# First tile of x on one queue with later loads held, first normalisations by column halves, first VectorE sums in other places

## The chip, the cores and the metric

One core of one Trainium2 chip. The metric is device time in microseconds (us), the median of several runs. The engines are named as in the profile: PE is TensorE (PEld its weight loads), DVE VectorE, ACT ScalarE, POOL GpSimd, SP SyncE, which issues most of the transfers. An engine works through its instructions in the order in which the program lists them.

## What is computed

x holds 2048 rows of 512 numbers (2 x 1024 x 512), all in fp32:

```python
xn = layernorm(x)                                  # per row, eps 1e-5
s  = xn @ (weight * block_mask).T                  # 512 x 512, 32 x 32 blocks
nx = xn * rsqrt(mean(xn * xn) + 1e-5) * ln_w
h  = silu(nx @ gate_w.T) * (nx @ up_w.T)           # 512 -> 1792
g  = silu(h @ down_w.T)                            # 1792 -> 512
out = x + s * g
```

## The kernel before, in words

**Tiling.** Rows are taken in four tiles `t` of 512, each as four pieces `i` of 128 rows by 512 columns (256 KB). A piece is normalised in place, transposed on PE by 128 x 128 blocks, and the four blocks of one column block `c` fill one PSUM bank `pt[t, c]`. From there ScalarE copies it out (`evacuate`, L158), or VectorE reads the bank directly in a sum.

**The products.** All matrix products are made by a scheme of seven products in place of eight, used twice, an outer one (`q`) over large blocks and an inner one (`m`) over small ones. It trades PE work for sums and differences of blocks, which VectorE and GpSimd make. `instance(j, ...)` (L333) is one outer product, with its seven inner ones in the order m = 1, 5, 2, 6, 3, 7, 4. Each inner product here is two matmul steps of 128 x 128 by 512, about 0.86 us together. They gather in banks `x`, `y` and `z` of the instance. After some of them a running value is copied away (`snap`, L358) or added to a total (`total`, L365). `seed` (L346) saves the first value of `x` as `s1` for the first two instances. `inner_b(q, m)` (L211) makes the operand sums of the x side, `inner_a` (L312) those of the weights, after `scale_a` (L266) has multiplied the weights by `ln_w`. Instances 0 and 1 need x tiles 0 and 1 only; tiles 2 and 3 come much later. The gate, up and attention products are 56 instances; after them come the down products (`down_instance`, L584) and the final sum.

**What sets the order.** Nothing is scheduled by the compiler. `at(pos, fn)` (L68) puts a function at a position; at the end all are called in the order of position, and ties in the order of entry. One position is one inner product, so instance j begins at 7 j. For the start, `T(us)` (L677) turns microseconds into positions, and `EARLY` (L678) moves the first products and sums of instances 0 and 1 to positions of their own. Waits follow from the data: whoever touches a buffer later waits for whoever touched it before.

**Names and lines that matter.**
- `load_x` (L118) issues the four pieces of a tile, for tile 0 two on SyncE and two on ScalarE. L681 to L691 list the first loads in SyncE's order: x tile 0, `ln_w`, weights of group 0 (two loads of 256 KB, `load_a`), x tile 1, weights of group 1, x tile 2, weights of group 2, x tile 3. `load_a` writes into the slots from `a1`.
- `constants` (L107) makes the identity matrix and others on GpSimd.
- `stats` (L124) is a bn_stats and a bn_aggr on VectorE for each piece; `factors` (L129) turns a tile's means and variances into scale and bias: VectorE, a square root on ScalarE, then two small VectorE instructions.
- `normalise` (L143) is one instruction for each piece, on ScalarE for pieces 0 and 1 and on VectorE for pieces 2 and 3.
- `RINGS` (L72) names the SBUF slots. `slot(tag)` takes them in turn; the rings `s2` and `s5` have two slots each, for the values that `snap` saves. `PSB` (L91) gives the PSUM banks: three for X, two for Y, one for Z, two for V. The first z of instance 1 lies in a Y bank, and so do `pt[0, 1]` and `pt[0, 2]`.
- `warm` (L698) is a row of products on the identity before the first data.

Of the kernel before, what the change touches and what calls it, by code (L numbers as in the profile page):

```python
# [10 lines left out]
AF = mybir.ActivationFunctionType  # L11
ALU = mybir.AluOpType
AX = mybir.AxisListType

P = 128
W = 512
# [15 lines left out]
def tile_masked_linear_gated_ffn(  # L32
# [35 lines left out]
    def at(pos, fn, *args):  # L68
        events.append((pos, len(events), fn, args))
# [23 lines left out]
    def bank(tag, name):  # L93
        return ps.tile([P, W], F32, tag=tag, name=name, bufs=PSB[tag])
# [23 lines left out]
    def load_x(t):  # L118
        for i in range(TT):
            xt[t, i] = mem[:, first_slot[("B6", "vc", "v5", "B4")[t]] + i, :]  # L120
            eng = nc.scalar if t == 0 and i >= 2 else nc.sync
            eng.dma_start(xt[t, i], x[(t * TT + i) * P : (t * TT + i + 1) * P, :])

    def stats(t, i):  # L124
        st = small.tile([P, 6], F32, tag="st", name=f"st_{t}_{i}")
# [14 lines left out]
        return [lambda: nc.vector.tensor_scalar(scl, agg[:, t, :, 1], 1.0 + EPS, EPS * EPS, ALU.mult, ALU.add),  # L140
                lambda: nc.scalar.activation(scl, scl, AF.Sqrt), last]

    def normalise(t, i, eng):  # L143
        scl, nb = stat[t]
        if eng is dve:
            nc.vector.tensor_scalar(xt[t, i], xt[t, i], scl[:, i : i + 1], nb[:, i : i + 1], ALU.mult, ALU.add)
            return
        nc.scalar.activation(xt[t, i], xt[t, i], AF.Identity, bias=nb[:, i : i + 1], scale=scl[:, i : i + 1])

    pt = {}  # L150

# [160 lines left out]
    def inner_a(g, part, k0=0, n=2):  # L312

        if part == 1:
            i, si, qs = F["a1"] + 2 * (g % 3), F["s"] + 2 * (g % 2), (1, 2)
        else:
            i, si, qs = *w_slots(g), BLOCKS
        a, s = slots(i + k0, n), slots(si + k0, n)
        a11, a21, a12, a22 = (a[:, :, k * P : (k + 1) * P] for k in range(4))
        s1, s2, s3, s4 = (s[:, :, k * P : (k + 1) * P] for k in range(4))  # L320
        for k in range(n):
            aop[g, qs[k0 + k]] = {1: a11[:, k], 2: a12[:, k], 3: s4[:, k], 4: a22[:, k],
                                  5: s1[:, k], 6: s2[:, k], 7: s3[:, k]}
        return [lambda: add(pool, s1, a21, a22), lambda: add(pool, s2, s1, a11, ALU.subtract),
                lambda: add(pool, s4, a12, s2, ALU.subtract), lambda: add(pool, s3, a11, a21, ALU.subtract)]
# [7 lines left out]
    def instance(j, g, q, prior, dest, after):  # L333


        st = {}

        seeded = j > 1

        def mm(m, tag, key, first):  # L340
            if first and key not in st:
                st[key] = bank("Y" if key == "z" and j == 1 else tag, f"{key}_{j}")
            nc.tensor.matmul(st[key], weights(g, q, m), operand(q, m), start=first and not (key == "z" and seeded),  # L343
                             stop=True, skip_group_check=True)

        def seed():  # L346

            if seeded:
                st["z"] = bank("Z", f"z_{j}")
                nc.scalar.copy(st["z"], st["x"])  # L350
            else:
                st["s1"] = slot("s2", f"s1_{j}")
                if prior is None:
                    nc.scalar.copy(st["s1"], st["x"])
                else:
                    add(dve, st["s1"], st["x"], prior(0))

        def snap(key, name, i):  # L358
            s = st[name] = slot(name, f"{name}_{j}")
            if prior is None:  # L360
                nc.scalar.copy(s, st[key])
            else:
                add(dve, s, st[key], prior(i))

        def total(key, name, i):  # L365
            if key == "z" and not seeded:
                name = "s1"
            if name:
                add(dve, dest(i), st[key], st[name])
            elif prior is None:  # L370
                nc.scalar.copy(dest(i), st[key])
            else:
                add(dve, dest(i), st[key], prior(i))

        at(EARLY.get((j, 0), 7 * j + 1), seed)
        for off, m, tag, first, snapshot, out in (
            (0, 1, "X", True, None, None),
            (2, 5, "Y", True, ("s5", 3), None),
            (3, 2, "Z", True, None, (None, 0)),
            (4, 6, "X", False, ("s2", 1), None),  # L380
            (6, 3, "Y", False, None, ("s2", 1)),
            (8, 7, "X", False, None, ("s5", 3)),
            (12, 4, "X", False, None, (None, 2)),
        ):
            key, pos = tag.lower(), 7 * j + off
# [198 lines left out]
    def down_instance(o, q, where_, prior, dest, after):  # L584
# [78 lines left out]
        if last_set:  # L663
            at(where_(17) + 0.1, base_of_last)
            for part, pos in zip(parts, (where_(23), where_(24), where_(25))):
# [8 lines left out]
    where = {gq: j for j, gq in enumerate(order)}  # L674
    N = len(order)
    END = 7 * N
    T = lambda us: (us - 14.9) / 0.86  # L677
    EARLY.update({(0, 1): T(11.5), (0, 0): T(12.6), (1, 1): T(12.7), (0, 2): T(12.8), (1, 2): T(12.9),  # L678
                  (1, 0): 4.5, (1, "z"): 7.0})
    SILU = 26.2  # L680
    at(T(-10), load_x, 0)  # L681
    at(T(-10), lambda: nc.sync.dma_start(lnw_sb, ln_w))
    for K in range(2):
        at(T(-10), load_a, 0, K)
    at(T(-10), load_x, 1)
# [3 lines left out]
    for K in range(2):  # L689
        at(T(-10), load_a, 2, K)  # L690
    at(T(-10), load_x, 3)  # L691
    at(T(-10), constants)
    def plan(pos, step, todo):
        for i, fn in enumerate(todo):
            at(pos + step * i, fn)


    def warm(n, b):  # L698
        for _ in range(n):
            nc.tensor.matmul(b[:, :P], ident, ident, start=True, stop=True, skip_group_check=True)  # L700

    at(T(1.4), lambda: warm(30, bank("V", "idle")))
    for t, p, step in ((0, T(8.2), 0), (1, T(13.4), 0), (2, 36.0, 1.2), (3, 36.1, 1.2)):
        plan(p, step, factors(t))
    for i in range(TT):
        half = act if i < 2 else dve
        at(T(4.5 + 0.85 * i), stats, 0, i)
        at(T(9.0 + 0.7 * (i % 2)), normalise, 0, i, half)
        at(T(10.1 + 0.8 * i), stats, 1, i)
        at(T(14.2 + 0.7 * (i % 2)), normalise, 1, i, half)  # L710
        for c in range(KC):
            at(T((10.2, 10.6, 11.0, 11.8)[c] + 0.1 * i), transpose, 0, c, (2, 3, 0, 1)[i], "XYYX"[c])
            at(T((15.3, 15.7, 16.1, 16.9)[c] + 0.1 * i), transpose, 1, c, (2, 3, 0, 1)[i], "XVVV"[c])
    at(T(6.0), scale_a, 0, 0, pool)
    at(T(8.2), scale_a, 0, 1, pool)
    for c in range(KC):
        at(T((10.7, 11.3, 11.9, 12.85)[c]), evacuate, 0, c, act)
        at((5.6, T(16.0), 6.0, 3.14)[c], evacuate, 1, c, act)
    for us, q, m, eng in ((15.9, 1, 5, dve), (16.6, 1, 6, dve), (17.2, 1, 7, dve), (17.8, 2, 5, dve), (18.4, 1, 4, pool),
                          (18.5, 2, 6, dve), (19.6, 2, 7, dve), (19.8, 2, 4, pool)):  # L720
        at(T(us), inner_b, q, m, eng)
    for q in (1, 2):
        for k in (0, 1):
            for n in (0, 1):
                at(8, outer_b, q, k, n, None)
    at(T(16.4), scale_a, 1, 0)
    at(5.2, scale_a, 1, 1)
    for i in range(TT):
        at(14.0 + 2.5 * i, stats, 2, i)
# [28 lines left out]
    for g in range(G + 1):  # L758
        p, rest = 7 * where[g, 1], 7 * where[g, BLOCKS[0]]
        for K in range(2):  # L760
            if g > 2:
                at(p - 22, load_a, g, K)
            if g == G:
                at(p - (10.4, 7.3)[K], lambda K=K: mask_a(aq[G, 0, K], 0, K))
            elif g > 1:
                at(p - (10.4, 7.3)[K], scale_a, g, K)
        if g:
            plan(p - 7, 1, inner_a(g, 1))
        else:
            plan(T(7.4), 0, inner_a(0, 1, 0, 1))  # L770
            plan(T(10.0), 0, inner_a(0, 1, 1, 1))
        at(rest - 29, load_block, g)

        def block_sums(g=g):
            for k, fn in enumerate(outer_a(g)):
                todo[g, k] = fn
        at(rest - 20, block_sums)
        if g == G:
            for k, (R, K) in ((1, (1, 0)), (4, (1, 1)), (0, (0, 0)), (3, (0, 1))):
                at(rest - 20.5, lambda k=k, R=R, K=K: mask_a(wblk[G][k], R, K))  # L780
        for k, off in enumerate((-19.9, -19.3, -18.1, -17, -15.95, -15.94, -15.93, -15.3, -13.95)):
            at(rest + off, lambda g=g, k=k: todo[g, k]())
        plan(rest - 13, 2.5, inner_a(g, 2, 0, 5))
# [138 lines left out]
```

## Time and profile before

| What | us |
|---|---|
| Median of 3 runs | 514.32 (514.15 to 514.35) |
| The profiled execution, own time | 514.33 |
| Its span, first to last instruction | 512.5 |
| Warm-up products on PE (L700), first start and busy time | 1.35, 8.37 |
| Factors of tile 0 on VectorE (L140), start | 8.06 |
| First transposes on PE (L155), start | 9.59 |
| The four early products `x`, `x`, `z`, `z` (L343), start | 11.59, 12.96, 13.82, 14.68 |
| The next ones `y`, `x`, `y`, `x`, `y`, start | 17.42, 18.97, 19.83, 20.96, 22.75 |
| Weight scaling on GpSimd (L262), two pairs, start | 6.89, 10.85 |
| Weight sums on GpSimd (L97), two sets of four, start | 8.80, 12.75 |

The table follows one execution through its first 23 us. Starts count from the span's start. The granted PE clock is full in all stages. The 1277 matmul records of the page are single steps; two of them make one inner product in the instances. PE records overlap, so a busy figure near the stretch's length means that one step follows another without a break, not that the array is at its peak. The transfers run without a break from 2.6 to about 17.5 us and then stop until 26; the 1.83 us between the span and the execution's own time lie around the program.

### The profile page before, as it was taken

What the parts mean: (1) busy time and instruction counts of PE and PEld (TensorE: products, weight loads), DVE (VectorE), ACT (ScalarE), POOL (GpSimd) and SP (SyncE); (2) the same over time, 40 slices, a digit from 0 to 9 for tenths busy, and PEclk for the clock granted to TensorE, in tenths of its full rate; (3) what the DMA queues carried; (4) which work ended last, traced back from release to release, by engine and by line L of the source; (5) the groups of instructions that cost most, each with busy time, mean ns of one, the idle gap of its engine ahead of it and who ended that gap; (6) DMA issues with size and microseconds to landing.
All of it is one profiled execution on the core that took longest, in us unless ns stands there. A gap on an engine that the chain in (4) does not pass through costs nothing. (4 is left out here: it accounts for less than half of the span.)

```text
span 512.5 us, 4939 instructions
## 1 busy us (share of the span) xinstructions
PE 506.2 (99%) x1277; PEld 231.2 (45%) x1277; DVE 380.8 (74%) x586; ACT 181.7 (35%) x344; POOL 340.5 (66%) x282
## 2 busy tenths in 40 slices
PE   8999999999999999999999999999999999999997
PEld 7444444444444444444444444444444444444444
DVE  5879689875987969789696978968847645367736
ACT  3566864642536344353634433331100101001111
POOL 5522223994695978869598789977652664739960
PEclk9999999999999999999999999999999999999999
DMA  8335645359159486685948567499997698467372
GB/s 310 142 123 215 245 156 217 153 226 329 60 220 334 165 297 233 230 299 209 315 181 296 205 246 258 156 334 390 352 345 269 198 382 320 146 255 220 145 230 83
DMA packets 60460, 121.59 MB, mean 237 GB/s; under 512 B 5760, under 2 KB 13328, under 8 KB 58384
## 3 DMA queue, kind: packets, MB, share of 16 engines
q1 hardware_dynamic: 60144, 120.75, 66.1%
q10 hardware_dynamic: 288, 0.52, 0.3%
q8 instruction: 10, 0.16, 0.1%
q14 instruction: 18, 0.15, 0.1%
HBM read 75.11 MB, written 46.15 MB: 237 GB/s over the span
## 5 line engine op out<-in xcount | busy, mean ns | idle before, releaser
L97 POOL TENSOR_TENSOR mem<-mem 128x512 f32<-128x512 f32 (+4 forms) x245 | 305.8, 1270 | 136.7 <-ACT mem L264 37.6
L343 PE MATMUL x<-mem 128*128 128x512 f32 x448 | 213.6, 594 | 0.3
L343 PEld LDWEIGHTS x<-mem 128*128 128x128 f32 x448 | 83.7, 190 | 106.9 <-issue 86.7
L97 DVE TENSOR_TENSOR mem<-x,mem 128x512 f32<-128x512 f32 x137 | 92.6, 684 | 42.2 <-PE x L343 41.1
L343 PE MATMUL y<-mem 128*128 128x512 f32 x224 | 114.6, 593 | 0.7 <-DVE mem L97 0.7
L97 DVE TENSOR_TENSOR mem<-mem 128x512 f32<-128x512 f32 (+3 forms) x60 | 75.6, 1266 | 7.2 <-PE dx L591 4.4
L591 PE MATMUL dx<-mem 128*128 128x512 f32 x174 | 78.3, 592 | 0.0
L97 DVE TENSOR_TENSOR mem<-y,mem 128x512 f32<-128x512 f32 x96 | 65.7, 684 | 10.0 <-PE y L343 8.7
L343 PEld LDWEIGHTS y<-mem 128*128 128x128 f32 x224 | 42.2, 190 | 53.3 <-issue 46.7
L350 ACT COPY z<-x 128x512 f32<-128x512 f32 x54 | 30.9, 573 | 97.8 <-PE x L343 93.3
L343 PE MATMUL z<-mem 128*128 128x512 f32 x112 | 57.1, 593 | 0.0
L591 PEld LDWEIGHTS dx<-mem 128*128 128x128 f32 x174 | 33.1, 190 | 41.6 <-issue 40.9
L591 PE MATMUL dy<-mem 128*128 128x512 f32 x98 | 44.5, 592 | 0.0
L409 ACT ACTIVATE gate<-mem 128x512 f32<-128x512 f32 x56 | 33.1, 601 | 25.4 <-DVE mem L97 21.0
L414 DVE TENSOR_TENSOR mem<-gate,mem 128x512 f32<-128x512 f32 x56 | 38.1, 681 | 5.1 <-POOL mem L97 4.3
L564 POOL TENSOR_TENSOR mem<-mem 128x512 f32<-128x512 f32 x16 | 24.3, 1516 | 15.4 <-DMA mem<-s_dram 15.1
L343 PEld LDWEIGHTS z<-mem 128*128 128x128 f32 x112 | 21.0, 190 | 25.3 <-issue 24.4
L574 ACT ACTIVATE silu<-mem 128x512 f32<-128x512 f32 x15 | 9.0, 602 | 64.6 <-DVE mem L97 48.3
L97 DVE TENSOR_TENSOR mem<-z,mem 128x512 f32<-128x512 f32 x41 | 28.0, 682 | 3.4 <-PE z L343 3.4
L591 PEld LDWEIGHTS dy<-mem 128*128 128x128 f32 x98 | 18.6, 190 | 23.4 <-issue 23.2
L97 DVE TENSOR_TENSOR mem<-dx,mem 128x512 f32<-128x512 f32 x16 | 11.0, 690 | 20.1 <-PE dx L591 20.1
L591 PE MATMUL dz<-mem 128*128 128x512 f32 x56 | 25.2, 592 | 0.0
(72 smaller groups left out, 286.8 us busy)
## 6 DMA issues: line engine op xcount, KB each, us to landing
h_dram<-mem SPq DMA_DIRECT2D x98, 256.0 KB, 2.1
mem<-h_dram SPq DMA_DIRECT2D x28, 768.0 KB, 6.7
mem<-in_gu SPq DMA_DIRECT2D x42, 256.0 KB, 4.0
acc_dram<-mem SPq DMA_DIRECT2D x8, 1024.0 KB, 4.1
mem<-acc_dram SPq DMA_DIRECT2D x8, 1024.0 KB, 6.0
s_dram<-mem SPq DMA_DIRECT2D x16, 256.0 KB, 4.4
mem<-s_dram SPq DMA_DIRECT2D x16, 256.0 KB, 6.7
mem<-in_x_t SPq DMA_DIRECT2D x16, 256.0 KB, 6.4
```

Source lines behind the costliest of these rows:

```text
L97: eng.tensor_tensor(o, a, b, op)
L343: nc.tensor.matmul(st[key], weights(g, q, m), operand(q, m), start=first and not (key == "z" and seeded), stop=True, skip_group_check=True)
L350: nc.scalar.copy(st["z"], st["x"])
L409: nc.scalar.activation(gate[key], t(), AF.Silu)
L414: nc.vector.tensor_mul(a(), gate[key], b())
L564: at_later.append(lambda: nc.gpsimd.tensor_tensor(s_tile, s_tile, rms_bc[t], ALU.mult))
L574: nc.scalar.activation(b[0][:, part], y[:, part] if source is None else source(), AF.Silu)
L591: nc.tensor.matmul(st[key], w(), b(), start=first and key != "z", stop=True, skip_group_check=True)
```

## The change

It has five parts, all in the first 23 us:
- All four pieces of x tile 0 are issued by SyncE; `ln_w` goes to ScalarE's queue. `constants` is listed first.
- GpSimd copies one column of piece 0 into the first `a1` slot. The first weight load, next on SyncE's queue, writes that slot and so waits until piece 0 has landed.
- `normalise` gets a range of columns. For tiles 0 and 1 it is called twice for each piece, for columns 0 to 255 and 256 to 511, first halves of both pieces before second halves.
- `s1` of instance 0 is taken from the ring `s5` instead of `s2`.
- Positions: `T` is shifted by 0.9 us, and the entries of the start are changed. The third early product is now m=1 of instance 1 and the second m=2 of instance 0. Both weight scalings stand before both sets of weight sums on GpSimd. On VectorE, the order after `inner_b(1, 5)`, `(1, 6)`, `(1, 7)` was `inner_b(2, 5)`, total of z 0, `inner_b(2, 6)`, s1 of instance 1, `inner_b(2, 7)`, total of y 0, total of z 1; it is now total of z 0, `inner_b(2, 5)`, s1 of instance 1, `inner_b(2, 6)`, total of z 1, total of y 0, `inner_b(2, 7)`. The warm-up has 26 products for 30.

```diff
-            eng = nc.scalar if t == 0 and i >= 2 else nc.sync
-            eng.dma_start(xt[t, i], x[(t * TT + i) * P : (t * TT + i + 1) * P, :])
+            nc.sync.dma_start(xt[t, i], x[(t * TT + i) * P : (t * TT + i + 1) * P, :])
...
-    def normalise(t, i, eng):
+    def normalise(t, i, eng, cols=slice(0, W)):
         scl, nb = stat[t]
+        v = xt[t, i][:, cols]
         if eng is dve:
-            nc.vector.tensor_scalar(xt[t, i], xt[t, i], scl[:, i : i + 1], nb[:, i : i + 1], ALU.mult, ALU.add)
+            nc.vector.tensor_scalar(v, v, scl[:, i : i + 1], nb[:, i : i + 1], ALU.mult, ALU.add)
             return
-        nc.scalar.activation(xt[t, i], xt[t, i], AF.Identity, bias=nb[:, i : i + 1], scale=scl[:, i : i + 1])
+        nc.scalar.activation(v, v, AF.Identity, bias=nb[:, i : i + 1], scale=scl[:, i : i + 1])
...
-                st["s1"] = slot("s2", f"s1_{j}")
+                st["s1"] = slot("s2" if j else "s5", f"s1_{j}")
...
-    T = lambda us: (us - 14.9) / 0.86
-    EARLY.update({(0, 1): T(11.5), (0, 0): T(12.6), (1, 1): T(12.7), (0, 2): T(12.8), (1, 2): T(12.9),
-                  (1, 0): 4.5, (1, "z"): 7.0})
+    T = lambda us: (us - 14.0) / 0.86
+    EARLY.update({(0, 1): T(10.4), (0, 2): T(11.3), (1, 1): T(12.1), (1, 2): T(13.0), (0, 0): T(11.5), (1, 0): 4.3,
+                  (0, "z"): 3.26, (1, "z"): 4.9})
     SILU = 26.2
+    at(T(-10), constants)
     at(T(-10), load_x, 0)
-    at(T(-10), lambda: nc.sync.dma_start(lnw_sb, ln_w))
+    at(T(-10), lambda: nc.scalar.dma_start(lnw_sb, ln_w))
+
+    at(T(-10), lambda: nc.gpsimd.tensor_copy(mem[:, F["a1"], 0:1], xt[0, 0][:, 0:1]))
...
-    at(T(1.4), lambda: warm(30, bank("V", "idle")))
-    for t, p, step in ((0, T(8.2), 0), (1, T(13.4), 0), (2, 36.0, 1.2), (3, 36.1, 1.2)):
+    at(T(1.4), lambda: warm(26, bank("V", "idle")))
+    for t, p, step in ((0, T(7.1), 0), (1, T(12.5), 0), (2, 36.0, 1.2), (3, 36.1, 1.2)):
...
-        at(T(4.5 + 0.85 * i), stats, 0, i)
-        at(T(9.0 + 0.7 * (i % 2)), normalise, 0, i, half)
-        at(T(10.1 + 0.8 * i), stats, 1, i)
-        at(T(14.2 + 0.7 * (i % 2)), normalise, 1, i, half)
+        at(T(3.7 + 0.82 * i), stats, 0, i)
+        at(T(9.35 + 0.82 * i), stats, 1, i)
+        for h, cols in enumerate((slice(0, W // 2), slice(W // 2, W))):
+            at(T(7.95 + 0.9 * h + 0.4 * (i % 2)), normalise, 0, i, half, cols)
+            at(T(13.45 + 0.9 * h + 0.4 * (i % 2)), normalise, 1, i, half, cols)
...
-    at(T(8.2), scale_a, 0, 1, pool)
+    at(T(6.1), scale_a, 0, 1, pool)
...
-        at((5.6, T(16.0), 6.0, 3.14)[c], evacuate, 1, c, act)
-    for us, q, m, eng in ((15.9, 1, 5, dve), (16.6, 1, 6, dve), (17.2, 1, 7, dve), (17.8, 2, 5, dve), (18.4, 1, 4, pool),
-                          (18.5, 2, 6, dve), (19.6, 2, 7, dve), (19.8, 2, 4, pool)):
-        at(T(us), inner_b, q, m, eng)
+        at((5.6, T(15.6), 6.0, 3.14)[c], evacuate, 1, c, act)
+    for pos, q, m, eng in ((1.1, 1, 5, dve), (1.87, 1, 6, dve), (2.56, 1, 7, dve), (3.95, 2, 5, dve), (2.7, 1, 4, pool),
+                           (4.6, 2, 6, dve), (7.2, 2, 7, dve), (5.0, 2, 4, pool)):
+        at(pos, inner_b, q, m, eng)
...
-    at(T(16.4), scale_a, 1, 0)
+    at(2.1, scale_a, 1, 0)
...
-            plan(T(7.4), 0, inner_a(0, 1, 0, 1))
-            plan(T(10.0), 0, inner_a(0, 1, 1, 1))
+            plan(T(9.9), 0, inner_a(0, 1, 0, 1))
+            plan(T(11.9), 0, inner_a(0, 1, 1, 1))
```

More of the change, by code (lines that the diff above doesn't have):

```diff
@@ L691, in tile_masked_linear_gated_ffn @@
     at(T(-10), load_x, 3)
-    at(T(-10), constants)
     def plan(pos, step, todo):
@@ L706, in tile_masked_linear_gated_ffn @@
         half = act if i < 2 else dve
-        at(T(4.5 + 0.85 * i), stats, 0, i)
-        at(T(9.0 + 0.7 * (i % 2)), normalise, 0, i, half)
-        at(T(10.1 + 0.8 * i), stats, 1, i)
-        at(T(14.2 + 0.7 * (i % 2)), normalise, 1, i, half)
+        at(T(3.7 + 0.82 * i), stats, 0, i)
[3 more added lines that the diff above has]
+            at(T(13.45 + 0.9 * h + 0.4 * (i % 2)), normalise, 1, i, half, cols)
         for c in range(KC):
-            at(T((10.2, 10.6, 11.0, 11.8)[c] + 0.1 * i), transpose, 0, c, (2, 3, 0, 1)[i], "XYYX"[c])
-            at(T((15.3, 15.7, 16.1, 16.9)[c] + 0.1 * i), transpose, 1, c, (2, 3, 0, 1)[i], "XVVV"[c])
+            at(T((8.9, 9.3, 9.8, 11.0)[c] + 0.05 * i), transpose, 0, c, (2, 3, 0, 1)[i], "XYYX"[c])
+            at(T((14.35, 14.8, 15.25, 16.2)[c] + 0.05 * i), transpose, 1, c, (2, 3, 0, 1)[i], "XVVV"[c])
     at(T(6.0), scale_a, 0, 0, pool)
-    at(T(8.2), scale_a, 0, 1, pool)
+    at(T(6.1), scale_a, 0, 1, pool)
     for c in range(KC):
-        at(T((10.7, 11.3, 11.9, 12.85)[c]), evacuate, 0, c, act)
-        at((5.6, T(16.0), 6.0, 3.14)[c], evacuate, 1, c, act)
-    for us, q, m, eng in ((15.9, 1, 5, dve), (16.6, 1, 6, dve), (17.2, 1, 7, dve), (17.8, 2, 5, dve), (18.4, 1, 4, pool),
-                          (18.5, 2, 6, dve), (19.6, 2, 7, dve), (19.8, 2, 4, pool)):
-        at(T(us), inner_b, q, m, eng)
+        at(T((9.75, 10.3, 10.85, 12.05)[c]), evacuate, 0, c, act)
+        at((5.6, T(15.6), 6.0, 3.14)[c], evacuate, 1, c, act)
+    for pos, q, m, eng in ((1.1, 1, 5, dve), (1.87, 1, 6, dve), (2.56, 1, 7, dve), (3.95, 2, 5, dve), (2.7, 1, 4, pool),
+                           (4.6, 2, 6, dve), (7.2, 2, 7, dve), (5.0, 2, 4, pool)):
+        at(pos, inner_b, q, m, eng)
     for q in (1, 2):
```

## The prediction

> **What bounds the kernel now.** First the page, for the span and the busiest engine; then the list of what TensorE waited for over the whole run; then busy time by stage.
>
> ```profile
> span 512.5 us, 4939 instructions
> PE 506.2 (99%) x1277; PEld 231.2 (45%) x1277; DVE 380.8 (74%) x586; ACT 181.7 (35%) x344; POOL 340.5 (66%) x282
> ```
>
> ```profile
> PE idle L700 <- POOL ident masks.py:199: 1.3, 1, 1.3
> PE y L343 <- DVE mem L97: 0.7, 1, 0.7
> PE pt L155 <- DVE mem L146: 0.3, 1, 0.3
> ```
>
> ```profile
> 17.40:22.75 5.35, 4.58 (x14) 1.70 (x13) 5.02 (x9) 4.63 (x10) 3.13 (x3) 1.00 0.03 8
> 22.75:325.00 302.25, 302.25 (x727) 134.22 (x728) 246.51 (x416) 142.64 (x275) 212.83 (x176) 1.00 0.62 222
> ```
>
> In the rows by stage the columns are the stretch, its length, the busy time of PE, PEld, DVE, ACT and POOL, the granted clock, the DMA share and GB/s. TensorE is busy in all 302.25 us after 22.75, and no later wait of it is listed. So the time is the moment at which this unbroken stream begins, plus a length that the change doesn't touch. The last wait, 0.7 us, ends at 22.75, where the ninth product `y` (instance 1, m=5; I write 1/5) begins. All of the argument is how early 1/5 can start. Next, therefore, VectorE and ScalarE in order of time from 4 to 40 us:
>
> ```profile
> 4.52 0.69 DVE L126 BATCH_NORM_STATS2 st<-mem 128x6 f32<-128x512 f32 x1 [4.52 <-DMA mem<-in_x]
> 5.53 0.69 DVE L126 BATCH_NORM_STATS2 st<-mem 128x6 f32<-128x512 f32 x1
> 8.97 1.17 DVE L146 TENSOR_SCALAR mem<-mem,scl,nb 128x512 f32<-128x512 f32 x2
> 10.06 0.68 DVE L126 BATCH_NORM_STATS2 st<-mem 128x6 f32<-128x512 f32 x1
> 14.74 1.01 DVE L146 TENSOR_SCALAR mem<-mem,scl,nb 128x512 f32<-128x512 f32 x2
> 16.68 0.69 DVE L97 TENSOR_TENSOR mem<-pt,mem 128x512 f32<-128x512 f32 x1 [0.93 <-PE pt L155]
> 17.73 0.69 DVE L97 TENSOR_TENSOR mem<-pt,mem 128x512 f32<-128x512 f32 x1 [0.36 <-ACT mem L163]
> 21.92 0.68 DVE L97 TENSOR_TENSOR mem<-y,mem 128x512 f32<-128x512 f32 x1
> 22.53 0.68 DVE L97 TENSOR_TENSOR mem<-z,mem 128x512 f32<-128x512 f32 x1
> ```
>
> ```profile
> 14.74 1.52 ACT L148 ACTIVATE mem<-mem,nb,scl 128x512 f32<-128x512 f32 x2 [0.73 <-DVE nb L138]
> 17.11 0.59 ACT L163 COPY mem<-pt 128x512 f32<-128x512 f32 x1 [0.85 <-PE pt L155]
> 17.60 0.91 ACT L264 ACTIVATE mem<-mem,lnw_sb 128x256 f32<-128x256 f32 x2
> 20.32 0.59 ACT L361 COPY mem<-x 128x512 f32<-128x512 f32 x1 [0.57 <-DVE mem L97]
> ```
>
> Backwards from 22.75. The `y` total of instance 0 runs 21.92 to 22.60 and 1/5 starts 0.15 us later. It is the ninth of VectorE's sums counted from the one at 16.68; they start one per 0.60 us without a gap from the second, at 17.73, the sum for m=6 (call it S6). S6 had to wait for ScalarE's copy of the same bank, 17.11 to 17.70. That copy waited for transposes, those for the second tile's normalisation from 14.74, that for four statistics from 10.06, those for VectorE's part of the first normalisation, and that for the first tile's statistics, which begin at 4.52 when the first 256 KB of x land. One chain, VectorE nearly all along it.
>
> [...] two queues at once moved about 400 GB/s from 2.7 us on, SyncE's alone 381 to 391 between 9 and 17 us. So one queue should lose no rate. [...] the trace's 256-column row (L264) has a mean of 0.504, and the normalisation of 512 a mean of 0.808. [...] No 256-column tensor_scalar of VectorE is in the trace.
>
> **The change part by part.** The sum is made against the profiled execution, 514.33 us (span 512.5 and 1.83 around it); the median of the runs is 514.32, so nothing is to be added.
>
> *One queue.* Before, two of the four x pieces are on SyncE's queue and two on ScalarE's, and two land together. The transfer view shows the first data in the slice at 2.6 us, 1.9 after the issue at 0.73, and the first statistics start at 4.52. At 400 GB/s, 256 KB is 0.65 us; without the other queue's piece beside it, 4.52 - 0.65 = 3.87. The bounds: 2.6 + 0.65 + 0.3 to signal = 3.55; and if it moves like a lone 256 KB read (the load issued at 31.64 moves data from 32.6 to 33.8 and lands 2.5 us after issue), 2.6 + 1.2 + 0.3 + 0.1 = 4.2. I take 3.9: **-0.6**. Also the second statistics began 1.01 us after the first, the others 0.79 to 0.83: its piece was late. One queue brings it 0.65 after the first, in time: **-0.2**. The lnw load moves to ScalarE's queue, 2 KB beside 1 MB: nothing. `constants` stays first on GpSimd.
>
> *The hold.* GpSimd copies one column of x into slot a1 after piece 0 lands; SyncE's next load overwrites that slot and waits. Behind it on SyncE are the second weight load, x tile 1 and everything later. GpSimd itself has only weight scaling next. Released near 4.1, the first weight load lands at 6.6 by the lone 2.5 us; the following ones 0.67 us apart (256 KB at 390 GB/s): second weights 7.3, x tile 1 from 7.9 to 9.9. Wanted: tile 1 at 9.4 for its first statistics and 11.8 for its last. The two scalings (1.83 us each, now both ahead of the sums) end near 10.3, wanted by the third early product near 12.7; the sums (2.06 each) at 12.4 and 14.3, wanted near 16.2 and 20.9. Covered by 1.5 us and more: 0. Beyond it, lateness of tile 1 costs its full amount.
>
> *First normalisation by halves.* VectorE issues four of 256 columns for two of 512. The 512 row has 0.558 us, a 4-column tensor_scalar 0.225 (L140); halfway is 0.39, spacing about 0.31, four of them some 1.3 us till the next statistics instead of 1.09: **+0.2**. Bounds: 0 if cost went with width alone, +0.8 if width were free. Earlier transposes here buy nothing: the four early products end at 15.4, beside the next normalisation, and move with it.
>
> *Second normalisation by halves.* With N its start: ScalarE's two first halves end at N + 0.40 + 0.50 = 0.90 (before: N + 1.52), all four at N + 1.7. Transposes of columns 0 to 127 finish at about N + 1.22, of 128 to 255 at N + 1.66, the copy of that bank starts at N + 1.75 and S6 at N + 2.36; before, 17.73 - 14.74 = 2.99. **-0.6**. VectorE's own four end at N + 1.3, ahead of its first sum at N + 1.4.
>
> *Order of sums, and the s1 slot.* The `z` total of instance 1 moves from tenth to eighth, before the `y` total of instance 0. Which matters for 1/5? It needs a Y bank, and both were last held by these two. Before, it started at 22.75, after the `y` total (22.60) and before the `z` total's end (23.21): it had the bank released first in program order. The `z` total is now the first to release, so 1/5 waits for the eighth sum, one spacing sooner: **-0.6**. s1 in s5 takes away ScalarE's 0.57 us wait before 20.32 (the snapshot of x waited for the `z` total that still read the s2 slot); alone it gives nothing, since VectorE's queue ends later, but TensorE must keep up: S6 + 0.75 transposes, + 0.5, three products of 0.86, end at S6 + 3.8; 1/5 is freed at S6 + 6 x 0.60 + 0.68 + 0.15 = S6 + 4.4. What is late next is the total of x before 0/4: eleventh, nine places after S6, freed at S6 + 9 x 0.60 + 0.83 = 6.2, and TensorE gets there at 6.15. So no new stall of note. The second-block sum moved to tenth is needed only at 1/7.
>
> *Warm-up of 26 for 30.* 60 records took 8.37 us, so 52 end near 8.6, when the first halves are ready at 8.5: 0.
>
> Sum: -0.6 - 0.2 + 0.2 - 0.6 - 0.6 = -1.8, giving **512.5**. S6 falls at 16.5, 1/5 at 20.95.
>
> **Rivals.**
> - *The bank is not the `z` total's.* 1/5 waits for the `y` total, ninth as before: -1.2, 513.1. For: I infer the allocator's rule from one start. Against: taking the last-released or a fixed bank contradicts that start.
> - *Halves don't act as halves* because transposes wait for both halves of a tile. Then the last half ends N + 1.7 for N + 1.52: +0.2 in place of -0.6, total -1.0, 513.3. Nothing in the trace shows waits by part of a slot on this path.
> - *The first piece comes no sooner* (latency, not sharing): -1.2, 513.1. For: 1.9 us pass before any data.
> - *Slower: one queue doesn't fill the DMA engines at the start.* At the lone read's 1.2 us per piece, ten pieces (x tile 0, two weights, x tile 1) end at 2.6 + 12 + 0.3 = 14.9, and tile 1's last statistics start 2.5 us later than the 12.46 of before; with -1.2 from the later parts, +1.3: 515.6. It decides from 1.07 us per piece on. Against: SyncE alone at 390 GB/s, 0.67 per piece.
>
> **How the numbers follow.** Likeliest 0.64 (own range 511.9 to 513.1: the first piece ±0.35, the halves -0.2 to +0.6 on VectorE); bank 0.14; halves 0.08; first piece 0.08; slower 0.06. A measurement of this kernel tells 0.2%, 1.03 us, from no change, so faster means below 513.29. Of the likeliest 0.60 lies there, of bank and first piece 0.08 and 0.05, of halves 0.03: faster 0.76, within 0.18 and slower 0.06. Range 511.9 to 513.4.
>
> **What would show it.** First statistics near 3.9, then an even 0.8 spacing; second statistics block at about 9.4; S6 near 16.5; 1/5 near 20.95, right behind a `z` total; TensorE without waits after it. Wrong: no earlier first statistics; a wait of VectorE on DMA before tile 1; transposes of the first columns that wait for the last half; 1/5 behind a `y` total; or a new wait of TensorE after 25 us.

## The result, and the profile after

| | before | after |
|---|---|---|
| Median, us (10 runs each) | 514.21 (513.99 to 514.54) | 513.17 (512.68 to 513.34) |
| Profiled execution, us | 514.33 | 513.17 |
| Its span | 512.5 | 511.4 |
| 1/5 starts | 22.75 | 21.55 |

The ratio after to before is 0.9978, with a 95% interval of 0.9969 to 0.9987: faster by 1.04 us in the medians, where 1.8 was forecast. First the page and the list of TensorE's waits, of after:

```profile
span 511.4 us, 4943 instructions
...
PE 505.8 (99%) x1269; PEld 231.8 (45%) x1269; DVE 380.4 (74%) x590; ACT 182.6 (36%) x348; POOL 340.9 (67%) x283
```

```profile
PE idle L702 <- POOL ident masks.py:199: 1.3, 1, 1.3
PE y L343 <- DVE mem L97: 0.3, 1, 0.3
PE x L343 <- DVE mem L97: 0.2, 1, 0.2
```

TensorE works without a listed wait from 1/5 on until the last of the three, which stands far behind the start:

```profile
326.19 1.12 PE L343 MATMUL x<-mem 128*128 128x512 f32 x2 [0.15 <-DVE mem L97]
```

This is a new wait after 25 us, which the prediction named as a sign of being wrong; it is 0.15 us long, and four of the later profiles have it too. But for it the time is once more the moment of 1/5. The timeline of after on VectorE (start, duration, engine, line, operation, operands, in brackets the idle time before it and what ended it):

```profile
3.56 0.69 DVE L125 BATCH_NORM_STATS2 st<-mem 128x6 f32<-128x512 f32 x1 [3.56 <-DMA mem<-in_x]
...
4.39 0.66 DVE L125 BATCH_NORM_STATS2 st<-mem 128x6 f32<-128x512 f32 x1
...
7.74 1.76 DVE L146 TENSOR_SCALAR mem<-mem,scl,nb 128x256 f32<-128x256 f32 x4
9.43 0.67 DVE L125 BATCH_NORM_STATS2 st<-mem 128x6 f32<-128x512 f32 x1
...
12.73 0.38 DVE L139 TENSOR_SCALAR scl<-agg 128x4 f32<-128x4 f32 x1
13.83 0.18 DVE L136 RECIPROCAL scl<-scl 128x4 f32<-128x4 f32 x1 [0.71 <-ACT scl L140]
...
14.24 1.59 DVE L146 TENSOR_SCALAR mem<-mem,scl,nb 128x256 f32<-128x256 f32 x4
...
17.12 0.69 DVE L97 TENSOR_TENSOR mem<-pt,mem 128x512 f32<-128x512 f32 x1 [0.36 <-ACT mem L163]
...
20.72 0.68 DVE L97 TENSOR_TENSOR mem<-z,mem 128x512 f32<-128x512 f32 x1
```

The same of after on ScalarE, and then on TensorE:

```profile
13.10 0.59 ACT L163 COPY mem<-pt 128x512 f32<-128x512 f32 x1
13.58 0.22 ACT L140 ACTIVATE scl<-scl 128x4 f32<-128x4 f32 x1
14.24 2.08 ACT L148 ACTIVATE mem<-mem,nb,scl 128x256 f32<-128x256 f32 x4 [0.44 <-DVE nb L137]
16.51 0.58 ACT L163 COPY mem<-pt 128x512 f32<-128x512 f32 x1 [0.19 <-PE pt L155]
```

```profile
1.35 8.98 PE L702 MATMUL idle<-ident 128*128 128x128 f32 x52 [1.35 <-POOL ident masks.py:199]
10.16 1.47 PE L155 MATMUL pt<-ident,mem 128*128 128x128 f32 x12
11.48 1.10 PE L343 MATMUL x<-mem 128*128 128x512 f32 x2
...
14.57 1.02 PE L343 MATMUL z<-mem 128*128 128x512 f32 x2
15.43 1.47 PE L155 MATMUL pt<-ident,mem 128*128 128x128 f32 x12
...
21.55 1.10 PE L343 MATMUL y<-mem 128*128 128x512 f32 x2 [0.34 <-DVE mem L97]
```

Three things are to be seen. The first statistics start 0.96 us sooner, and half of that is gone again at the start of the second normalisation (N from here on): 14.24 for 14.74. VectorE stood still for 0.71 us before its reciprocal at 13.83, where before it had been 0.27: the input of the square root was ready at 12.73 + 0.38 = 13.11, but ScalarE's square root came at 13.58, right behind the copy of the fourth transposed bank. The rows of before for these two:

```profile
13.38 0.39 DVE L140 TENSOR_SCALAR scl<-agg 128x4 f32<-128x4 f32 x1
14.04 0.18 DVE L137 RECIPROCAL scl<-scl 128x4 f32<-128x4 f32 x1 [0.27 <-ACT scl L141]
```

And the warm-up, eight records shorter than before, took longer: 8.98 us for 8.37. It ended at 10.33, though the first halves, begun at 7.74 and 7.79, were all done by about 8.9, so transposes, early products and ScalarE's copies all began late.

Why a shorter warm-up takes longer is seen in its records by microsecond. The rows of before, of the warm-up line alone (stretch, length, busy time and count of matmul records, granted clock, DMA share, GB/s):

```profile
3.00:4.00 1.00, 1.00 (x6) 1.00 1.06 406
4.00:5.00 1.00, 1.00 (x10) 1.00 1.04 404
5.00:6.00 1.00, 1.00 (x12) 1.00 1.10 389
```

And of after:

```profile
5.00:6.00 1.00, 1.00 (x7) 1.00 0.70 193
6.00:7.00 1.00, 1.00 (x6) 1.00 1.04 389
7.00:8.00 1.00, 1.00 (x9) 1.00 0.86 264
8.00:9.00 1.00, 1.00 (x11) 1.00 0.95 358
```

A slice has 6 to 7 records at first and 11 or 12 later. Records that lie across an edge count in both slices; from start to start it is 0.21 us at first and 0.11 us later. The change comes at 4.3 us in this profile of before, at 7.5 in that of after. The granted clock reads 1.00 on both sides, so only the rate shows it. What brings the change about is not shown. The 14 profiles of this study have it anywhere from 4.3 to 7.5 us, which is 2.9 to 6.1 us after the first product at 1.35, and this range is what counts here.

### The profile page after: what moved, and what is told of

Same layout as the page of the kernel before. It is cut to its first block, busy times and chain, and to the rows that moved or that the text cites. A ratio compares the mean times of both kernels' runs of the same rounds, so it can differ in the third digit from the quotient of the medians.

```text
span 511.4 us, 4943 instructions
## 1 busy us (share of the span) xinstructions
PE 505.8 (99%) x1269; PEld 231.8 (45%) x1269; DVE 380.4 (74%) x590; ACT 182.6 (36%) x348; POOL 340.9 (67%) x283
```

## The experiments

Two readings of the missing 0.7 us were set against each other. By the first, the warm-up and what stands behind it (transposes, copies, the square root in ScalarE's order) hold the start back, so that neither the earlier x nor the halves can show. By the second, only VectorE's own chain counts, and its halves cost more than they bring. Ratios below are against the kernel before on the same chip. A single profile is uncertain by 0.2 to 0.3 us at these points, as the repeat `a_again` shows, and by more where a piece of x lands late.

**Fewer warm-up products**, on the kernel after:

```diff
-    at(T(1.4), lambda: warm(26, bank("V", "idle")))
+    at(T(1.4), lambda: warm(20, bank("V", "idle")))
```

> The changed kernel with 20 warm-up products for 26. Theory W (the warm-up row holds up the first transposes, so tile 0's products end late and its copies on ScalarE stand before tile 1's square root): warm-up ends near 6.5 to 8.0, first transposes start near 8.2 for 10.16, the first product x near 10.2 for 11.48, the square root of tile 1 no longer waits (13.1 for 13.58), S6 at about 16.6 for 17.12, product 1/5 at about 21.0 for 21.55, and the time some 0.5 us below the changed kernel's 513.17. Rival R (only VectorE's chain counts, as in the prediction): early products come sooner, S6 and the time stay within 0.2 us of the changed kernel.

Measured: 513.22 us, ratio 0.9978 (0.9971 to 0.9985). In its profile the warm-up ends at 8.14, the first transposes start at 8.65, the first product at 10.80, and the square root no longer waits for a copy. But VectorE waited 0.23 us for the third piece of x, N stayed at 14.24, and 1/5 started at 21.33. The 0.5 us that the first reading expected isn't there: the time can't be told from that of the kernel after.

**Tile 0 by whole pieces**, on the kernel after:

```diff
+        at(T(7.95 + 0.4 * (i % 2)), normalise, 0, i, half)
         for h, cols in enumerate((slice(0, W // 2), slice(W // 2, W))):
-            at(T(7.95 + 0.9 * h + 0.4 * (i % 2)), normalise, 0, i, half, cols)
```

> The changed kernel with tile 0 normalised in whole pieces again, tile 1 by halves. Both theories: VectorE's first normalisation takes 1.1 us for 1.7, tile 1's statistics start at about 8.9 for 9.43. Theory W: the square root of tile 1 still stands behind ScalarE's copies, which the warm-up delays, so S6 moves by less than 0.15 us and the time stays. Rival R: S6 and product 1/5 come 0.5 us sooner, time about 512.6.

Measured: 513.08 us, 0.9974 (0.9965 to 0.9983). From the start of VectorE's part to the next statistics it took 1.22 us, where the kernel after took 1.69. Two late pieces (0.51 and 0.23 us) used that up in the profile, N being 14.69. The time stays, as the first reading expected, but not for its reason: here the warm-up ended at 9.66, and the square root waited for its input, not for a copy. This kernel can't be told from the kernel after either.

**The loads alone**, on the kernel before (one queue, `ln_w` on ScalarE's queue, the hold, the earlier scaling), and the same with 20 warm-up products:

```diff
-            eng = nc.scalar if t == 0 and i >= 2 else nc.sync
-            eng.dma_start(xt[t, i], x[(t * TT + i) * P : (t * TT + i + 1) * P, :])
+            nc.sync.dma_start(xt[t, i], x[(t * TT + i) * P : (t * TT + i + 1) * P, :])
...
+    at(T(-10), constants)
     at(T(-10), load_x, 0)
-    at(T(-10), lambda: nc.sync.dma_start(lnw_sb, ln_w))
+    at(T(-10), lambda: nc.scalar.dma_start(lnw_sb, ln_w))
+    at(T(-10), lambda: nc.gpsimd.tensor_copy(mem[:, F["a1"], 0:1], xt[0, 0][:, 0:1]))
...
-    at(T(8.2), scale_a, 0, 1, pool)
+    at(T(6.1), scale_a, 0, 1, pool)
```

> The kernel before with the loads part alone (x tile 0 on one queue, lnw on ScalarE's, the hold) and both weight scalings ahead of the sums; whole normalisations, old order of sums, 30 warm-up products. Both: first statistics near 3.6 for 4.52, tile 0's factors near 6.9 for 8.06. Theory W: the 30 warm-up products end at 9.7 at best and near 10.9 where the array speeds up late, so the first product x starts at 11.4 to 12.7, the square root of tile 1 stays near 13.8, and the time is within 0.3 us of the kernel before, or up to 1 us above it. Rival R: everything moves by 1.1 us, time about 513.1.

> The same with 20 warm-up products for 30. Theory W: the warm-up is out of the way, first product x near 10.5, square root of tile 1 near 12.7, time about 1.0 us below the kernel before. Rival R: the same as with 30, within 0.2 us.

Measured: 513.92 us, 0.9993 (0.9985 to 1.0001), and with 20 products 513.86, 0.9988 (0.9981 to 0.9994). The loads brought the first statistics to 3.60, 0.9 us sooner. About half of that reached the end in the first profile: N is 14.20 for 14.74, and 1/5 starts at 22.28 for 22.75; the median is 0.52 us below that of the kernel before there, though the interval reaches 1. The input of the square root was ready at 12.81, the square root ran at 13.33 behind the copies, and VectorE stood for 0.77 us. In the second the square root came after 0.04 us, but a piece of x was 0.67 us late, and N fell at 14.34. Neither reading has this pair right. The second expected 513.1 and the first next to nothing for the loads; the first expected 20 products to bring the time 1.0 us below the kernel before, where it is 0.58 below and the two medians are 0.06 us apart.

**The order of sums and the s1 slot alone**, on the kernel before:

```diff
-                st["s1"] = slot("s2", f"s1_{j}")
+                st["s1"] = slot("s2" if j else "s5", f"s1_{j}")
...
-                  (1, 0): 4.5, (1, "z"): 7.0})
+                  (1, 0): 4.3, (0, "z"): 3.26, (1, "z"): 4.9})
...
-    for us, q, m, eng in ((15.9, 1, 5, dve), (16.6, 1, 6, dve), (17.2, 1, 7, dve), (17.8, 2, 5, dve), (18.4, 1, 4, pool),
-                          (18.5, 2, 6, dve), (19.6, 2, 7, dve), (19.8, 2, 4, pool)):
-        at(T(us), inner_b, q, m, eng)
+    for pos, q, m, eng in ((1.16, 1, 5, dve), (1.98, 1, 6, dve), (2.67, 1, 7, dve), (3.95, 2, 5, dve), (4.07, 1, 4, pool),
+                           (4.6, 2, 6, dve), (7.2, 2, 7, dve), (5.7, 2, 4, pool)):
+        at(pos, inner_b, q, m, eng)
```

> The kernel before with only the new order of VectorE's first sums and s1 of instance 0 in s5; loads, normalisations and warm-up as before. The prediction's step: S6 stays near 17.7 and product 1/5 starts right behind the z total of instance 1, now eighth, at about 22.15 for 22.75; time 0.6 us below the kernel before. Rival (the bank comes from the y total): 1/5 stays near 22.75 and the time within 0.2 us.

Measured: 513.84 us, 0.9992 (0.9983 to 1.0000). VectorE and TensorE in its profile:

```profile
17.66 0.69 DVE L97 TENSOR_TENSOR mem<-pt,mem 128x512 f32<-128x512 f32 x1 [0.36 <-ACT mem L163]
...
21.26 0.68 DVE L97 TENSOR_TENSOR mem<-z,mem 128x512 f32<-128x512 f32 x1
21.86 0.68 DVE L97 TENSOR_TENSOR mem<-y,mem 128x512 f32<-128x512 f32 x1
```

```profile
22.09 1.10 PE L343 MATMUL y<-mem 128*128 128x512 f32 x2 [0.36 <-DVE mem L97]
```

S6 is where it was before (17.66 for 17.73), and 1/5 starts 0.15 us after the end of the `z` total, at S6 + 4.43 for S6 + 5.02, with the `y` total still running. The bank is the `z` total's, and the term is 0.6 us. The median shows 0.44 of it.

**Without the hold**, and **tile 1 by whole pieces**, each on the kernel after:

```diff
-    at(T(-10), lambda: nc.gpsimd.tensor_copy(mem[:, F["a1"], 0:1], xt[0, 0][:, 0:1]))
```

```diff
+        at(T(13.45 + 0.4 * (i % 2)), normalise, 1, i, half)
         for h, cols in enumerate((slice(0, W // 2), slice(W // 2, W))):
...
-            at(T(13.45 + 0.9 * h + 0.4 * (i % 2)), normalise, 1, i, half, cols)
```

> The changed kernel without GpSimd's one-column copy, so that nothing holds the weight loads and x tile 1 behind piece 0. Theory Q (one queue alone gives the early first piece, the hold is not needed): first statistics still near 3.6, the pieces behind it no later, first weights land near 6.2 for 7.4, time within 0.3 us of the changed kernel. Rival H (the hold keeps the other loads off the first tile's): the third and fourth statistics wait 0.3 to 1 us for their pieces, and the time rises by as much.

> The changed kernel with tile 1 normalised in whole pieces, tile 0 by halves. The prediction's step: from the start of tile 1's normalisation to S6 3.0 us for 2.4, so 0.6 us later. What the changed kernel's profile suggests: 3.0 us for its measured 2.88, so S6, product 1/5 and the time 0.1 to 0.2 us later.

Measured: 513.56 us, 0.9986 (0.9979 to 0.9993), and 513.57, 0.9984 (0.9978 to 0.9991). Without the hold the first statistics start at 3.62, much as with it: it isn't what brings the first piece. From 5 to 6 us the transfers move 363 GB/s without it and 193 with it, so it leaves a hole; against that, VectorE waited 0.29 us for the fourth piece without it. The intervals of both overlap with that of the kernel after, so what the hold is worth stays open. With whole pieces in tile 1, S6 fell at N + 3.04, and TensorE waited 0.68 us for VectorE's piece before its transposes. By halves, six profiles have N + 2.58 to N + 2.88. The halves of tile 1 thus bring 0.2 to 0.5 us at S6.

The profile without the hold also shows what the price of a half hangs on. Its VectorE halves of tile 0 and of tile 1, and GpSimd's work at that time:

```profile
8.21 2.02 DVE L146 TENSOR_SCALAR mem<-mem,scl,nb 128x256 f32<-128x256 f32 x4
...
14.85 1.38 DVE L146 TENSOR_SCALAR mem<-mem,scl,nb 128x256 f32<-128x256 f32 x4
```

```profile
7.32 3.68 POOL L262 TENSOR_SCALAR mem<-mem,lnw_sb 128x256 f32<-128x256 f32 x4 [5.25 <-DMA mem<-in_gu]
10.97 3.82 POOL L97 TENSOR_TENSOR mem<-mem 128x128 f32<-128x128 f32 x8
```

The same four instructions take 2.02 us while GpSimd scales weights and 1.38 us after GpSimd's sums have ended at 14.79. All 14 profiles say the same of single records: a half takes 0.40 to 0.41 us with GpSimd idle (12 records) and 0.56 in the mean beside it (29 records), a whole piece 0.54 to 0.55 (6) and 0.68 (22). No run was made for this, so it is a difference that goes with GpSimd's work, not one shown by taking that work away.

**One edit: all x pieces on one queue**, the kernel before otherwise:

```diff
-            eng = nc.scalar if t == 0 and i >= 2 else nc.sync
-            eng.dma_start(xt[t, i], x[(t * TT + i) * P : (t * TT + i + 1) * P, :])
+            nc.sync.dma_start(xt[t, i], x[(t * TT + i) * P : (t * TT + i + 1) * P, :])
```

> The kernel before with the two x pieces of ScalarE's queue moved to SyncE's and nothing else: lnw behind them on SyncE, no hold. What is open is why the first data moved at 1.7 us in the changed kernel for 2.55 before. If two queues that issue at the same moment hold each other up: first data near 1.7, first statistics near 3.6. If it is the small lnw load on ScalarE's queue, or the hold: first data at 2.5, first statistics at 3.9 or later. Time 0 to 0.8 us below the kernel before.

Measured: 514.47 us, 0.9998 (0.9990 to 1.0006). Its VectorE, ScalarE and TensorE:

```profile
3.22 0.69 DVE L125 BATCH_NORM_STATS2 st<-mem 128x6 f32<-128x512 f32 x1 [3.22 <-DMA mem<-in_x]
...
11.97 0.42 DVE L139 TENSOR_SCALAR scl<-agg 128x4 f32<-128x4 f32 x1
14.21 0.18 DVE L136 RECIPROCAL scl<-scl 128x4 f32<-128x4 f32 x1 [1.82 <-ACT scl L140]
```

```profile
11.19 1.56 ACT L162 COPY mem<-pt 128x512 f32<-128x512 f32 x3 [2.23 <-PE pt L154]
13.00 0.59 ACT L353 COPY mem<-x 128x512 f32<-128x512 f32 x1 [0.26 <-PE x L342]
13.48 0.59 ACT L162 COPY mem<-pt 128x512 f32<-128x512 f32 x1
13.96 0.22 ACT L140 ACTIVATE scl<-scl 128x4 f32<-128x4 f32 x1
```

```profile
10.55 1.47 PE L154 MATMUL pt<-ident,mem 128*128 128x128 f32 x12
```

The statistics came 1.3 us sooner, and tile 1's variance was ready at 12.39. Then VectorE stood for 1.82 us: the square root waited its turn behind ScalarE's copies, these for transposes that began at 10.55, as the warm-up ended. ScalarE had been idle for 2.23 us before its first copy. All of the 1.3 us was lost in this queue; N was 14.89, 0.15 later than before, and 1/5 started at 22.90. The median of twelve runs agrees: it is 0.09 us above that of the kernel before there. With this the reading by VectorE's chain alone falls.

**The kernel after once more**, and **20 warm-up products with tile 0 whole** (the two edits above together):

> The changed kernel once more, unedited, beside the next three on one chip. Theory W+D (the time of the start is set by when pieces 2 and 3 of x tile 0 land and by when the array speeds up, both of which differ from run to run): the median 0.2% below the kernel before as in the first measurement, but the profile shows another first product x (10.6 to 11.6), another warm-up end, and VectorE's third or fourth statistics waiting up to 0.7 us. Rival: the profile of before 23 us repeats within 0.1 us.

> The changed kernel with tile 0 in whole pieces and 20 warm-up products, nothing else. Theory W (warm-up and halves of tile 0 both cost, and each hides the other): where the third and fourth pieces are on time, the square root of tile 1 at 12.9 for 13.58, S6 near 16.4 for 17.12, time 0.5 us below the changed kernel. Rival: within 0.2 us of it.

Measured: 513.01 us, 0.9974 (0.9964 to 0.9984), and 512.82, 0.9970 (0.9958 to 0.9982). Together the two edits take the copies out of the way (the square root runs at 13.07, when its input is there), N comes to 14.01 and 1/5 to 21.19, where the repeat of the kernel after has 14.10 and 21.38. The time is 0.19 us below that of the repeat, where the first reading expected 0.5 and its rival at most 0.2.

Three times, then, 20 warm-up products stood in place of 26 or 30 with nothing else changed. The ratios went from 0.9978 to 0.9978, from 0.9993 to 0.9988, and from 0.9974 to 0.9970 (`a_whole0` and this kernel), partly on different chips. What the late warm-up does is seen in the profiles, as an order of waits; in the times it is not shown. No run moves the square root ahead of the copies, which would be the direct trial.

**A version that goes further.** The first try was this, with the two edits above:

```diff
-    EARLY.update({(0, 1): T(10.4), (0, 2): T(11.3), (1, 1): T(12.1), (1, 2): T(13.0), (0, 0): T(11.5), (1, 0): 4.3,
-                  (0, "z"): 3.26, (1, "z"): 4.9})
+    EARLY.update({(0, 1): T(10.4), (0, 2): T(11.3), (1, 1): T(12.1), (1, 2): T(13.0), (0, 0): T(11.5), (1, 0): 2.6,
+                  (0, "z"): 2.3, (1, "z"): 3.3})
...
-            at(T((14.35, 14.8, 15.25, 16.2)[c] + 0.05 * i), transpose, 1, c, (2, 3, 0, 1)[i], "XVVV"[c])
+            at((T(14.35), T(14.8), T(15.25), 4.1)[c] + 0.06 * i, transpose, 1, c, (2, 3, 0, 1)[i], "XVVV"[c])
...
-        at((5.6, T(15.6), 6.0, 3.14)[c], evacuate, 1, c, act)
+        at((5.6, 1.9, 6.0, 5.1)[c], evacuate, 1, c, act)
-    for pos, q, m, eng in ((1.1, 1, 5, dve), (1.87, 1, 6, dve), (2.56, 1, 7, dve), (3.95, 2, 5, dve), (2.7, 1, 4, pool),
-                           (4.6, 2, 6, dve), (7.2, 2, 7, dve), (5.0, 2, 4, pool)):
+    for pos, q, m, eng in ((1.1, 1, 5, dve), (1.87, 1, 6, dve), (3.0, 1, 7, dve), (3.6, 2, 5, dve), (2.7, 1, 4, pool),
+                           (4.5, 2, 6, dve), (12.5, 2, 7, dve), (5.0, 2, 4, pool)):
...
-    at(2.1, scale_a, 1, 0)
+    at(5.15, scale_a, 1, 0)
```

The copy of tile 1's second bank goes behind S6, and both `z` totals before the two sums that read the last transposed bank, `inner_b(2, 5)` and `(2, 6)`.

> The changed kernel with 20 warm-up products, tile 0 in whole pieces, ScalarE's copy of the second bank of tile 1 behind S6 instead of ahead of it, the last transposes of tile 1 and two of ScalarE's later instructions (copy of that bank, a weight scaling) further back, and VectorE's sums in the order (1,5), (1,6), total z 0, s1 of instance 1, (1,7), total z 1, (2,5), (2,6), totals of y 0 and x 0, the two snapshots, (2,7). If the chain from S6 to product 1/5 is VectorE's queue, as the prediction has it: S6 2.2 us after the start of tile 1's normalisation for 2.88, 1/5 3.9 us after S6 for 4.43, the time about 1.2 us below the changed kernel. If something else holds 1/5 back, the time stays within 0.3 us of it, or TensorE shows a new wait.

Measured: 513.61 us, 0.9986 (0.9979 to 0.9993). S6 came at N + 2.65, and a new wait ate the gain, here on TensorE:

```profile
20.19 0.44 PE L155 MATMUL pt<-ident,mem 128*128 128x128 f32 x2 [1.06 <-DVE mem L97]
```

Two of the last transposes stood behind the `z` total of instance 1, which writes into the slot of the first piece of x tile 1; TensorE lost 1.06 us. In this order the total comes before the transpose that reads that piece, so the kernel doesn't compute what is asked for 128 rows, and its time stands only for the wait. The second try puts these transposes, and product 0/6 before them, ahead of that total, and keeps the halves of tile 1 on ScalarE alone:

```diff
-            at(T((14.35), T(14.8), T(15.25), 4.1)[c] + 0.06 * i, transpose, 1, c, (2, 3, 0, 1)[i], "XVVV"[c])
+            at((T(14.35), T(14.8), T(15.25), 3.1)[c] + 0.06 * i, transpose, 1, c, (2, 3, 0, 1)[i], "XVVV"[c])
...
-                  (0, "z"): 2.3, (1, "z"): 3.3})
+                  (0, "z"): 2.3, (1, "z"): 3.35, (0, 6): 3.0})
...
+            if i < 2:
+                at(T(13.45 + 0.9 * h + 0.4 * (i % 2)), normalise, 1, i, half, cols)
+            elif h == 0:
+                at(T(13.45 + 0.4 * (i % 2)), normalise, 1, i, half)
```

> The changed kernel with 20 warm-up products, tile 0 in whole pieces, tile 1 by halves on ScalarE only, ScalarE's copy of tile 1's second bank behind S6, product 0/6 ahead of tile 1's last transposes, those ahead of the z total of instance 1, and VectorE's sums as in a_reorder. In a_reorder that total overwrote a quarter of one piece of x tile 1 before its transpose, so that kernel computes other values for 128 rows, and the transposes waited 1.06 us for the total; here the order is right. If product 1/5 hangs on VectorE's queue: S6 2.3 us after the start of tile 1's normalisation, 1/5 4.0 us after S6, at 20.6 to 21.0, no wait of the transposes, time about 0.7 us below the changed kernel and 1.7 below the one before. If the gain is taken back by something later: within 0.3 us of the changed kernel, with a new wait of TensorE.

Measured: 512.63 us, 0.9966 (0.9953 to 0.9978), the least of all. TensorE in its profile, and the list of TensorE's waits:

```profile
10.46 1.10 PE L343 MATMUL x<-mem 128*128 128x512 f32 x2
...
15.43 1.42 PE L155 MATMUL pt<-ident,mem 128*128 128x128 f32 x11 [0.21 <-DVE mem L146]
...
20.80 1.07 PE L343 MATMUL y<-mem 128*128 128x512 f32 x2
```

```profile
PE idle L702 <- POOL ident masks.py:199: 1.4, 1, 1.4
PE pt L155 <- DVE mem L146: 0.8, 3, 0.4
```

1/5 starts at 20.80 without a wait for any sum; from the transposes at 15.43 on no wait of TensorE is listed, so these now set it. S6 came at N + 2.80, not at the N + 2.3 expected, since VectorE's whole pieces ended only at N + 1.36 and the transposes waited for them. On the chip of these runs this version lies from 512.41 to 512.93 us (five runs), the kernel after from 512.76 to 513.49 (eight), and the intervals of their ratios overlap. The medians are 0.38 us apart, where 0.7 was expected.

## Why the prediction was right in direction, and 0.7 us off in size

The prediction put S6 at 16.5 and 1/5 at 20.95; in the profile of after they are at 17.12 and 21.55. The miss is all ahead of S6. What the prediction had right is that the time follows 1/5, and the reason for the order of sums. By its steps:

- **One queue, -0.6:** -0.96; the first statistics start at 3.56, the early edge of the bounds of 3.55 to 4.2. Sharing was not the whole of it: by 2.5 us transfers had moved some 150 KB in after and none in before. The further 0.36 us had no reason in the prediction and is luck.
- **The second statistics' gap, -0.2:** -0.18, as worked out.
- **The hold, 0:** no cost in the profile of after, but its cover is thinner than the 1.5 us given. The first weights landed at 7.50, not at 6.6, and in three other profiles with one queue VectorE waited 0.2 to 0.65 us for a piece of tile 1.
- **First normalisation by halves, +0.2:** +0.60 (1.69 us to the next statistics for 1.09), inside the bound of +0.8. A 256-column instruction of after has a mean of 0.478 us, where 0.39 was taken. The 0.39 is right for a half with GpSimd idle (0.40 to 0.41), and wrong here, where GpSimd scales weights all through the four halves (7.50 to 11.18). The 0.558 from which it was worked out is the middle of four records of before, two beside GpSimd's work (0.57 and 0.68) and two not (0.55 and 0.54).
- **Warm-up, 0:** this is the step whose reasoning failed, though in the sum it is the smaller part of the miss. "60 records took 8.37 us, so 52 end near 8.6" takes a mean over two rates. The eight records left out were of the quick kind, about 0.9 us in all, and the change of rate, which the profile of before shows only once, came 3.2 us later. In 3.2 us at the slow rate (0.21 us a record) TensorE does what takes 1.7 at the quick one (0.11), a loss of 1.5: 9.72 - 0.9 + 1.5 is the end at 10.33. With it fell the sentence that earlier transposes buy nothing because the early products "move with it": ScalarE's copies behind those transposes stand before the square root. VectorE's wait for it rose by 0.44 us. The bias instruction next on VectorE took 0.16 for 0.45, which gave back 0.29. That too is luck, and goes with GpSimd: in before this instruction starts 0.02 us after a weight sum on GpSimd (14.23 to 14.69) and ends with it, in after it starts at 14.04, ahead of the next one at 14.11. In twelve of the 14 profiles it ends within 0.03 us of the end of such a sum. From the second statistics to N it is +0.13, where the prediction had 0.
- **Second normalisation by halves, -0.6:** -0.11. Of the missing half microsecond, 0.3 is ScalarE: its four halves took 2.08 us for 1.7, each 0.590 where 0.504 was taken. The 0.504 is the mean of the 256-column weight scaling (L264) in before, and was too low for this form. In `a_warm20`, where TensorE was free in time, the bank's copy starts right at the end of these four, at N + 2.05, and S6 is N + 2.67. The other 0.2 is TensorE: in after the transposes start at 15.43, N + 1.19, right behind the last early product, which began 0.86 us before, the spacing of these products. That is the warm-up again, since the last early product begins at 13.55 in the last version, for 14.57.
- **Order of sums, -0.6:** -0.59 (S6 + 4.43 for S6 + 5.02), right also in its reason, as `b_sums` shows by itself. The total of x before 0/4, which it named as next in line, makes no listed wait, as forecast.

Added up against the profile of before: -0.96 and -0.18, +0.60, a remainder of -0.09 in the first factors, +0.13, -0.11 and -0.59 make -1.20, and 22.75 becomes 21.55. The terms missed partly cancel: the first piece gave 0.36 more than forecast, and the halves of both tiles and the wait for ScalarE 1.0 less. The range of 511.9 to 513.4 held the time; without the 0.36 us of the first piece it would not have. Of the rivals, the bank's is refuted by `b_sums`, the one in which halves don't act as halves by the transposes of after, which start at 15.43 while ScalarE's second halves run until 16.32, the late first piece by every run with one queue, and the slower one too, since tile 1's statistics began sooner than before in all but one of those runs (10.14 in `a_nohold`, for 10.06). The slower rival's place was wrong; a stall of that kind came, but on ScalarE's queue.

Shown: that the order of sums is worth 0.6 us at 1/5, and, in the profile and the times of `b_onequeue`, that an earlier first tile can be lost whole in ScalarE's queue behind a late warm-up. In `b_loads` half of it got through. Only argued: how much of the 0.7 us the warm-up, the two halves' terms and GpSimd's work beside them would each give back alone. Single runs differ by as much, and the kernels with one part taken back don't separate in time from the kernel after.

## What to carry to other kernels

When a chain hops to another engine for one small instruction, read what stands ahead of that instruction in the other engine's order, and how late it can become, before an earlier start is counted as gain: in `b_onequeue` VectorE stood for 1.82 us that way. Fill such as warm-up products has a rate of its own, here 0.21 us a record at first and 0.11 later: read it by stretches, not as a mean, and look for its end in more than one profile. Cutting an instruction in two is to be priced from the same form on the same engine, with the same neighbour at work: with GpSimd at work a half took 0.56 us here for 0.40.

## What the runs showed of the hardware that had not been expected

- TensorE's change from 0.21 to 0.11 us between the starts of small matmuls came between 4.3 and 7.5 us in the 14 profiles, with TensorE busy from 1.35 on in all of them, and with a granted clock of 1.00 in the records throughout.
- VectorE's normalising instructions took 0.40 us for 256 columns and 0.54 for 512 with GpSimd idle, and 0.56 and 0.68 in the mean with GpSimd at work.
- With four pieces of x on one queue the first statistics began at 3.22 to 3.70 us in twelve profiles, with two pieces each on two queues at 4.52 and 4.45 in two. With one queue data first moved at 1.7 to 1.9 us; in before none did until 2.5. But two queues don't always begin so late: `b_sums` has the loads of before, and its rows (as above, of the warm-up line) show data, and then none.

```profile
1.60:2.00 0.40, 0.40 (x3) 1.00 0.35 118
2.00:2.40 0.40, 0.40 (x4) 1.00 0.00 0
```

The earlier statistics come neither from the hold nor from the place of `ln_w`: `b_onequeue` has no hold, leaves `ln_w` on SyncE's queue, and shows them too. Why little or nothing moves before 2.4 us with two queues stays open.
- In six of twelve profiles with one queue VectorE waited 0.2 to 0.7 us for some piece of x of the first two tiles. No edit goes with it.
